# Projections in quarters at even distances, checks moved to the last groups, and a shorter lead-in, in a fused graph attention and graph convolution kernel

## Chip, core and metric

The kernel runs on one core of one Trainium2 chip. Its time is the device time of one execution in microseconds (us), given as a median of several runs. The core has five engines: PE (matrix multiplication), DVE (vector), ACT (activation functions), POOL (general purpose) and SP, which here issues DMA transfers. DVE and ACT read what PE leaves in PSUM; POOL does not.

## What is computed

Layer 0 is an attention over a graph of N = 2708 nodes with D = 128 features, with 128 "slices" of 8 components each; then come a residual, a layer norm and a two-step graph convolution. Only the attention matters here:

```python
q = (x @ Wq.T).reshape(d, n, h)      # d = 128 slices, n = 2708, h = 8
k = (x @ Wk.T).reshape(d, n, h)
v = (x @ Wv.T).reshape(d, n, h)
a = jnp.einsum('dnh,dmh->dnm', q, k) * scale
a = a + spatial_encoding + edge_encoding      # both are adj
a = jax.nn.softmax(a, axis=2)
out = jnp.einsum('dnm,dmh->dnh', a, v)
```

The reshape mixes tokens and slices. 128 tokens of x (a chunk) give 128 x 128 rows of q, k and v, in the order in which the slices use them; four slices need 4 x 2708 = 10832 rows. So the first chunk of tokens (16384 rows) holds all that the first four slices need, the second is first needed by the next four, and so on.

## The kernel before, in words

**Groups and steps.** Four slices are a group (`GB`), and there are 32 groups. A group goes through six blocks of 452 queries, and a block through 9 steps of a plan, so a group has 54 steps and the kernel 1728. A step has two to four **pieces** and one **two-exponential chunk**. A piece is two 128 x 452 tiles of transposed scores: PE multiplies (`score`, L415, into the PSUM tile `s`, two buffers), DVE adds the adjacency (`add_near`, L422, into a part of `e`, five buffers), and after the last piece ACT takes exp(2 x) of all of them in one instruction (L518). For the chunk named in `TWO_EXP`, three of the four tiles go another way: PE leaves scores in the PSUM tile `p`, ACT takes the exponential (L515, into `w`), and POOL multiplies by a ready exp(2 adj) (L516, `w<-w,ecol`). PE then multiplies `e` and `w` by the values (`add_up`, L432 to L440), and DVE copies a finished block out (`hand_on`, L446).

**exp(2 adj).** In group 0 ACT computes it, one 128 x 452 tile a step (`first_exp`, L397), and SP stores it to DRAM (`near_exp`); later groups load it (`ecol`). `look_at_near` (L404) takes, on DVE, the minimum of each of the 54 tiles in groups 0 to 3 and the maximum in groups 4 to 7. At the end, both decide with other checks whether a slower, safer attention has to be run.

**Projections.** Those of the first two token chunks (`FIRST = 2`) run before all else, K, Q and V in turn. The other 20 chunks are cut into halves of 512 columns, 120 in all, placed "amid" the steps: every sixth step in group 0, and before steps 2, 10, 18 and 26 of each later group. A half is one matmul call (two matmuls in the trace, L343) into an `s` buffer, an eviction on DVE (L345), for K and Q a cast and a subtraction on POOL (L356, L357) and two stores by SP (L352), for V one store (L347). These jobs stand in a list; one is taken at the second piece of each step. The last job of a half loads the weights of the next (L335, tile `wc`, one buffer).

**Other loads.** SP issues all DMAs, in program order: adjacency tiles eight loads ahead (`load_adj`), queries of the next block, and over the 54 steps of a group the keys and values of the next group (`load_keys`, 16 DMAs into 8 partitions each, at even steps to 30; `load_values`). POOL reorders the keys at odd steps from 33 to 49 (`order_keys`, L262) and spreads the values at steps 50 to 53.

**Order.** The order of the work on PE is not by hand: `interleave` is a planner that keeps a rough clock of PE, ACT, DVE and POOL from constants (the cost of a score, a product, a projection) and yields pieces, products and projections. The engines then run in that order and wait on semaphores.

The functions that the diff touches, with line numbers:

Of the kernel before, what the change touches and what calls it, by code (L numbers as in the profile page):

```python
# [18 lines left out]
P = 128  # L19
H = 8  # L20
# [19 lines left out]
def interleave(plan, blocks, short, amid=(), bufs=4, patience=0.1):  # L40
# [10 lines left out]
    PROJECT, TAKE, SPLIT = 0.95, 0.7, 1.25  # L51
# [91 lines left out]
def graph_attention_gcn(ctx: ExitStack, tc: tile.TileContext, x, xT, adj, adjT, adjP, adjS,  # L143
# [45 lines left out]
    with ExitStack() as s:  # L189
# [58 lines left out]
        def load_keys(g, h):  # L248


            if h == 0:
                groups[g] = kpool.tile([P, NU, P], F32R, tag="k", name="k"), k_short[g % 2], vals[g % 2], v_short[g % 2]
                raw_keys[g] = raw.tile([P, N], F32R, tag="k_raw", name="k_raw")
            nc.sync.dma_start(raw_keys[g][ds(H * h, H), :].bitcast(F32),
                              ks[ds(H * (h % 4 // 2), H), ds((GB * g + h // 4) * N, N)])
# [26 lines left out]
        def load_q(g, b):  # L282
            n0, nw = QBS[b]
            q = queries[g, b] = qpool.tile([P, QB], F32R, tag="q", name="q")
            for j in range(GB):
                for i in range(2):
                    nc.sync.dma_start(q[ds(32 * j + 2 * H * i, 2 * H), :nw].bitcast(F32),
                                      qs[:, ds((GB * g + j) * N + n0, nw)])
# [31 lines left out]
        assert GB * N <= FIRST * P * P  # L320
        halves = [(c, i, h) for c in range(FIRST, NM) for i in range(3) for h in range(2)]
# [6 lines left out]
        def load_half(n):  # L328
            c, i, h = halves[n]
# [4 lines left out]
            given[c, i, h] = proj.tile([P, NB], F32, tag="wc", name="wc")  # L334
            nc.sync.dma_start(given[c, i, h], projections[i][0][:, ts(h, NB)])  # L335

        def project(n):

            c, i, h = halves[n]
# [3 lines left out]
            nc.tensor.matmul(pp[:mi, 0, :], given[c][:, :mi], given.pop((c, i, h)), start=True, stop=True)  # L343
            a = proj.tile([P, NB], F32, tag="pa", name="pa")[:mi]
            nc.vector.tensor_scalar_mul(a, pp[:mi, 0], half_scale if i == 1 else 1.0)  # L345
            if i == 2:
                return [lambda: nc.sync.dma_start(dst.rearrange("(i g) e -> i (g e)", g=P)[ds(i0, mi), ts(h, NB)], a)]  # L347
            o = proj.tile([P, 2, NB], F32R, tag="pr", name="pr")[:mi]

            def store():  # L350
                for l in range(2):
                    nc.sync.dma_start(dst.rearrange("r (i g) -> i r g", g=P)[ds(i0, mi), ds(H * l + 4 * h, 4)],  # L352
                                      o[:, l].bitcast(F32).rearrange("p (e g) -> p e g", g=P))


            return [lambda: nc.gpsimd.tensor_copy(o[:, 0], a),  # L356
                    lambda: nc.gpsimd.tensor_sub(o[:, 1], a, o[:, 0].bitcast(F32)), store]  # L357
# [6 lines left out]
        for n in range(ahead):  # L364
            load_adj(n)
        load_half(0)
        for i, (_, dst) in enumerate(projections):
            for c in range(FIRST):
                pp = ps.tile([P, 2, NB], F32, tag="s", name="s")
                for h in range(2):  # L370
                    nc.tensor.matmul(pp[:, h, :], first_x[:, ts(c, P)], first_w[:, ts(2 * i + h, NB)], start=True, stop=True)
                o = flat(epool.tile([P, 8, QB], F32, tag="e", name="e"))[:, : 4 * NB].rearrange("p (l f) -> p l f", l=2)
                if i == 2:
                    nc.scalar.copy(o[:, 0], flat(pp))
                    nc.sync.dma_start(dst.rearrange("(i g) e -> i (g e)", g=P)[ts(c, P)], o[:, 0])
                else:
                    f = half_scale if i == 1 else 1.0
                    nc.scalar.mul(o[:, 0].bitcast(F32R), flat(pp), f)
                    nc.vector.scalar_tensor_tensor(o[:, 1].bitcast(F32R), flat(pp), f, o[:, 0], ALU.mult, ALU.subtract)
                    nc.sync.dma_start(dst.rearrange("r (i g) -> i r g", g=P)[ts(c, P)],  # L380
                                      o.rearrange("p l (e g) -> p (l e) g", g=P))
            if i == 1:
                for h in range(16):
                    load_keys(0, h)
                load_q(0, 0)
        for j in range(GB):
            load_values(0, j)
        for h in range(9):
# [4 lines left out]
        def first_exp(b, m):  # L393
# [3 lines left out]
            nc.scalar.activation(t[:, :nw], adj_cols[0, b, -1 - m][:, :nw], AF.Exp, scale=2.0)  # L397
# [3 lines left out]
        def look_at_near(g, b, m):  # L401
            x = TWO_EXP.index(m)
            if g < 8 and g % 4 == x % 4:
                nc.vector.tensor_reduce(ends[:, g // 4, ds(b * len(TWO_EXP) + x, 1)], exp_cols[g, b, m][:, : QBS[b][1]],  # L404
                                        AX.X, (ALU.min, ALU.max)[g // 4])
# [45 lines left out]

        amid = list(range(2, 54, 6)) + [54 * g + t for g in range(1, NG) for t in (2, 10, 18, 26)]
        amid = amid[: len(halves)]
        for g in range(1, NG):
            c = (min(NG, g + 2) * GB * N - 1) // (P * P)
            assert c < FIRST or amid[halves.index((c, 2, 1))] + 8 < 54 * g
        jobs = []
        loaded = ahead
        for what, n, c, beside in interleave(plan, len(steps) // len(plan), NU, amid, bufs=5):
            if what == "amid":  # L460
                at = amid.index(n)
                jobs += project(at)
                if at + 1 < len(halves):
                    jobs.append(lambda n=at + 1: load_half(n))
# [369 lines left out]
```

## Time and profile before

| | |
|---|---|
| median of 3 runs | 6900.82 us (6892.52 to 6908.93) |
| profiled execution, its own time | 6904.39 us |
| its span in the profile | 6902.6 us |
| lead-in, to the first POOL product | 50 us |
| attention, 32 groups | to 6561 us |
| layer norm and convolution | the last 341 us |
| busy, share of the span | PE 96%, ACT 94%, DVE 89%, POOL 83% |
| ACT busy by group | 200.2 us of 200.2 in group 29; 226.8 of 238.8 in group 0 |
| checks L404 | 108 x 0.615 us (median) on DVE, from 50.7 to 1715.3 us |
| first exponentials L397 | 54 x 0.577 us (median) on ACT, in group 0 |
| evictions of halves L345 | 120, 0.691 us each at 128 rows |

Times are from one profiled execution. A row of the profile names a line of the code, its engine, and output and input by the program's names; "idle before" and the name after an arrow are the wait just ahead of an instruction and what ended it. PE's busy time is modelled and should not be read as a share of its peak. A group is told by POOL's products: every 54th starts one.

### The profile page before, as it was taken

To read this page: it belongs to the slowest core of one execution; us is meant where nothing else is said; L and a number is where in the kernel's file an instruction comes from. 1 tells how busy PE (TensorE), PEld (TensorE's weight loads), DVE (VectorE), ACT (ScalarE), POOL (GpSimd) and SP (SyncE) were. 2 spreads that over 40 slices of the span, in tenths; PEclk is the share of its full clock that TensorE was granted. 3 is DMA by queue.
4 is the path that set the end of the run, shared out by engine and by line. 5 is a ranking of instruction groups with operands and counts; after the bars stand their busy time and mean duration, and the time that the engine had idled before them with its cause. 6 is when DMAs were issued, how large, how long until landed. Compare 5 with 4: busy or idle time off the path is not lost.

```text
span 6902.6 us, 137500 instructions
## 1 busy us (share of the span) xinstructions
PE 6641.2 (96%) x50426; PEld 1983.7 (29%) x50426; DVE 6112.2 (89%) x6307; ACT 6501.8 (94%) x3605; POOL 5761.7 (83%) x2546
## 2 busy tenths in 40 slices
PE   7999999999999999999999999999999999999979
PEld 2222222222222222222222222222222222222254
DVE  6899999999999999999999999999999999999941
ACT  7999999999999999999999999999999999999910
POOL 5888888888888989888898988889898888888800
PEclk8999999999999999999999999999999999999999
DMA  8888887878888888888878788877888887777667
GB/s 266 269 246 243 249 239 234 246 241 242 249 245 243 243 246 245 253 246 247 241 242 249 245 251 248 248 240 243 244 244 255 247 240 232 231 235 239 199 203 232
DMA packets 1143258, 1674.16 MB, mean 243 GB/s; under 512 B 148922, under 2 KB 1090366, under 8 KB 1138478
## 3 DMA queue, kind: packets, MB, share of 16 engines
q1 hardware_dynamic: 1142574, 1665.29, 79.7%
q8 instruction: 399, 6.54, 0.4%
q14 instruction: 285, 2.33, 0.1%
HBM read 1582.90 MB, written 81.80 MB: 241 GB/s over the span
## 4 chain that ended last, share of the span: by engine, by line
PE 54%; DMA 13%; DVE 12%; POOL 8%; issue 6%; ACT 4%; SPq 3%; DVEq 0%; POOLq 0%; ACTq 0%
PE acc L440 27%; PE s L415 18%; DVE e L422 11%; POOL w L516 7%; DMA col<-in_adjP 4%; PE acc L661 3%; ACT w L515 2%; DMA k_raw<-ks 2%; PE p L415 2%; ACT e L518 2%; PE acc L437 2%; DMA two<-in_adjP 2%; DMA ecol<-ne 1%; PE s L343 1%; DMA q<-qs 1%
## 5 line engine op out<-in xcount | busy, mean ns | idle before, releaser
L516 POOL TENSOR_TENSOR w<-w,ecol 128x1356 f32<-128x1356 f32 (+1 forms) x1728 | 5347.4, 3102 | 755.0 <-ACT w L515 622.6
L422 DVE TENSOR_TENSOR e<-s,col 128x904 f32<-128x904 f32 (+1 forms) x4608 | 4831.3, 1092 | 339.9 <-PE s L415 196.8
L518 ACT ACTIVATE e<-e 128x2712 f32<-128x2712 f32 (+5 forms) x1728 | 4747.6, 2747 | 17.4 <-DVE e L422 14.8
L440 PE MATMUL acc<-e,vals 128*9 128x452 f32 x20352 | 3553.2, 545 | 0.1
L415 PE MATMUL s<-q,k 32*128 32x452 f32 x10944 | 2501.3, 462 | 183.4 <-DVE e L422 117.7
L515 ACT ACTIVATE w<-p 128x1356 f32<-128x1356 f32 (+1 forms) x1728 | 2439.2, 1412 | 47.1 <-PE p L415 28.5
L415 PEld LDWEIGHTS s<-q,k 32*128 32x128 f32 x10944 | 1016.7, 182 | 3370.6 <-DVE e L422 2979.4
L440 PE MATMUL acc<-w,vals 128*9 128x452 f32 x10368 | 1622.6, 545 | 0.0
L415 PE MATMUL p<-q,k 32*128 32x452 f32 (+1 forms) x5184 | 1400.5, 446 | 18.7 <-ACT w L515 18.4
L422 DVE TENSOR_TENSOR e<-s,two 128x904 f32<-128x904 f32 (+1 forms) x960 | 1049.1, 1093 | 119.9 <-PE s L415 61.1
L440 PEld LDWEIGHTS acc<-e,vals 128*9 128x9 f32 x20352 | 452.0, 89 | 807.7 <-issue 805.8
L415 PEld LDWEIGHTS p<-q,k 32*128 32x128 f32 x5184 | 575.5, 182 | 63.9 <-ACT w L515 53.6
L440 PEld LDWEIGHTS acc<-w,vals 128*9 128x9 f32 x10368 | 200.9, 88 | 193.2 <-issue 177.5
L262 POOL CAST k<-k_raw 128x336 fp32r<-128x336 f32 x251 | 222.3, 886 | 37.6 <-DMA q<-qs 37.6
L432 PE MATMUL acc<-e,v_short 128*128 128x452 f32 (+1 forms) x384 | 197.1, 595 | 0.0
L437 PE MATMUL acc<-e,v_first 128*32 128x452 f32 (+1 forms) x1536 | 185.9, 556 | 2.5
L343 PE MATMUL s<-wc,xc 128*128 128x512 f32 (+1 forms) x240 | 136.3, 650 | 6.4 <-DMA wc<-in_WvT 3.4
L345 DVE TENSOR_SCALAR pa<-s 128x512 f32<-128x512 f32 (+1 forms) x120 | 82.9, 691 | 48.6 <-PE s L343 46.2
L446 DVE COPY o<-acc 128x452 f32<-128x452 f32 x192 | 118.9, 619 | 6.4 <-PE acc L440 6.4
L661 PE MATMUL acc<-col,xw 128*128 128x512 f32 (+2 forms) x264 | 105.5, 549 | 0.0
L555 ACT ACTIVATE sd<-mv,eps 128x1 f32<-128x1 f32 (+1 forms) x22 | 6.0, 294 | 104.5 <-DVE mv L549 104.4
L661 PE MATMUL acc<-col,hw 128*128 128x512 f32 (+2 forms) x264 | 104.1, 545 | 0.0
(84 smaller groups left out, 1069.0 us busy)
## 6 DMA issues: line engine op xcount, KB each, us to landing
col<-in_adjP SPq DMA_DIRECT2D x1965, 226.0 KB
two<-in_adjP SPq DMA_DIRECT2D x1440, 226.0 KB
ecol<-ne SPq DMA_DIRECT2D x1395, 226.0 KB
col<-in_adjP SPq DMA_DIRECT2D x393, 224.0 KB
two<-in_adjP SPq DMA_DIRECT2D x288, 224.0 KB
ecol<-ne SPq DMA_DIRECT2D x279, 224.0 KB
col<-in_adjT SPq DMA_DIRECT2D x210, 256.0 KB
k_raw<-ks SPq DMA_DIRECT2D x512, 84.6 KB
```

The source lines that it names most:

```text
L262: copy(k[:, :, ts(i, n)], t[:, ts(i, n * NU)].rearrange("p (q c) -> p c q", c=NU))
L343: nc.tensor.matmul(pp[:mi, 0, :], given[c][:, :mi], given.pop((c, i, h)), start=True, stop=True)
L415: nc.tensor.matmul(to[:, :nw], k[r, m, :], q[r], start=True, stop=True)
L422: nc.vector.tensor_add(e[:, ds(at, 2), :nw], st[:, :, :nw], a)
L432: nc.tensor.matmul(a[:, :nw], vz, e[:, t, :nw], start=False, stop=False)
L437: nc.tensor.matmul(a[ds(32 * j, 32), :nw], v_first[g % 2][:, ds(32 * j, 32)], e[:, t, :nw], start=True, stop=False)
L440: nc.tensor.matmul(a[ds(32 * j, VW), :nw], v[:, m, ds(VW * j, VW)], e[:, t, :nw], start=False, stop=(m == last_chunk))
L446: nc.vector.tensor_copy(o[:, :nw], acc.pop((g, b))[:, :nw])
L515: nc.scalar.activation(w[:, :, :nw], sp[:, :, :nw], AF.Exp, scale=2.0)
L516: nc.gpsimd.tensor_mul(w[:, :, :nw], w[:, :, :nw], exp_cols[g, b, two][:, :nw].unsqueeze(1).to_broadcast([P, 3, nw]))
L518: nc.scalar.activation(e[:, :at, :nw], e[:, :at, :nw], AF.Exp, scale=2.0)
L661: nc.tensor.matmul(acc[:, :nw], src[:mw, m, :], t[:mw, :nw], start=(m == 0), stop=(last is None and m == NM - 1))
```

## The change

1. **Quarters.** Halves become quarters of 256 columns, 240 of them, each put at step 2 + 32 n // 5 for n = 0 to 239, so every 6.4 steps to step 1531 (in group 28). Cast and subtraction of a quarter become one job; the load of the next stays the last job. The planner's constants for a projection are changed.
2. **Checks.** The minimum of exp(2 adj) is taken in the last three groups, 18 tiles in each. In place of the maximum, `first_exp` has ACT give the sum of each row with the exponential (`accum_out`).
3. **Lead-in.** Only chunk 0 is projected ahead of the first loads of keys and queries. Half of these loads are issued on ACT's queue. The projections of chunk 1 come after the loads of values. Of the eight adjacency loads ahead, two go out before the projections and six after V of chunk 0 is stored.

The diff, cut to its core:

```diff
-    PROJECT, TAKE, SPLIT = 0.95, 0.7, 1.25
+    PROJECT, TAKE, SPLIT = 0.5, 0.36, 1.0
...
-        def load_keys(g, h):
+        def load_keys(g, h, queue=nc.sync):
...
-            nc.sync.dma_start(raw_keys[g][ds(H * h, H), :].bitcast(F32),
+            queue.dma_start(raw_keys[g][ds(H * h, H), :].bitcast(F32),
...
-        assert GB * N <= FIRST * P * P
-        halves = [(c, i, h) for c in range(FIRST, NM) for i in range(3) for h in range(2)]
+        assert GB * N <= P * P
+        quarters = [(c, i, h) for c in range(FIRST, NM) for i in range(3) for h in range(4)]
+        QW = 2 * P
...
-            nc.tensor.matmul(pp[:mi, 0, :], given[c][:, :mi], given.pop((c, i, h)), start=True, stop=True)
-            a = proj.tile([P, NB], F32, tag="pa", name="pa")[:mi]
-            nc.vector.tensor_scalar_mul(a, pp[:mi, 0], half_scale if i == 1 else 1.0)
+            nc.tensor.matmul(pp[:mi, 0, :QW], given[c][:, :mi], given.pop((c, i, h)), start=True, stop=True)
+            a = proj.tile([P, QW], F32, tag="pa", name="pa")[:mi]
+            nc.vector.tensor_scalar_mul(a, pp[:mi, 0, :QW], half_scale if i == 1 else 1.0)
+
+            def load():
+                if n + 1 < len(quarters):
+                    load_quarter(n + 1)
+
             if i == 2:
-                return [lambda: nc.sync.dma_start(dst.rearrange("(i g) e -> i (g e)", g=P)[ds(i0, mi), ts(h, NB)], a)]
-            o = proj.tile([P, 2, NB], F32R, tag="pr", name="pr")[:mi]
+                to = dst.rearrange("(i g) e -> i (g e)", g=P)[ds(i0, mi), ts(h, QW)]
+                return [lambda: nc.sync.dma_start(to, a), load]
+            o = proj.tile([P, 2, QW], F32R, tag="pr", name="pr")[:mi]
+
+            def split():
+
+                nc.gpsimd.tensor_copy(o[:, 0], a)
+                nc.gpsimd.tensor_sub(o[:, 1], a, o[:, 0].bitcast(F32))
...
-            return [lambda: nc.gpsimd.tensor_copy(o[:, 0], a),
-                    lambda: nc.gpsimd.tensor_sub(o[:, 1], a, o[:, 0].bitcast(F32)), store]
+            return [split, store, load]
...
-        for n in range(ahead):
+        for n in range(2):
             load_adj(n)
-        load_half(0)
-        for i, (_, dst) in enumerate(projections):
-            for c in range(FIRST):
...
-            if i == 1:
-                for h in range(16):
-                    load_keys(0, h)
-                load_q(0, 0)
+
+        def project_all(c, i):
...
+        for i in range(2):
+            project_all(0, i)()
+        store_v = project_all(0, 2)
+        for h in range(16):
+            load_keys(0, h, nc.scalar if h % 2 else nc.sync)
+        load_q(0, 0, (nc.sync, nc.scalar))
+        store_v()
+        for n in range(2, ahead):
+            load_adj(n)
         for j in range(GB):
             load_values(0, j)
+        for i in range(3):
+            project_all(1, i)()
+        load_quarter(0)
         for h in range(9):
             order_keys(0, h, (nc.gpsimd.tensor_copy, nc.vector.tensor_copy, nc.scalar.copy)[h % 3])
...
-            nc.scalar.activation(t[:, :nw], adj_cols[0, b, -1 - m][:, :nw], AF.Exp, scale=2.0)
+            x = b * len(TWO_EXP) + TWO_EXP.index(m)
+            nc.scalar.activation(t[:, :nw], adj_cols[0, b, -1 - m][:, :nw], AF.Exp, scale=2.0,
+                                 accum_out=ends[:, 1, x : x + 1])
...
             x = TWO_EXP.index(m)
-            if g < 8 and g % 4 == x % 4:
-                nc.vector.tensor_reduce(ends[:, g // 4, ds(b * len(TWO_EXP) + x, 1)], exp_cols[g, b, m][:, : QBS[b][1]],
-                                        AX.X, (ALU.min, ALU.max)[g // 4])
+            if x % 3 == g - NG + 3:
+                nc.vector.tensor_reduce(ends[:, 0, ds(b * len(TWO_EXP) + x, 1)], exp_cols[g, b, m][:, : QBS[b][1]],
+                                        AX.X, ALU.min)
...
-        amid = list(range(2, 54, 6)) + [54 * g + t for g in range(1, NG) for t in (2, 10, 18, 26)]
-        amid = amid[: len(halves)]
+        amid = [2 + 32 * n // 5 for n in range(len(quarters))]
```

`project_all(c, i)` does for one chunk and one of K, Q and V what the two loops did: two matmuls, ACT's eviction, DVE's remainder for K and Q; it returns the store, so that it can be issued later.

## Prediction

> **What bounds the kernel now.** I first read the page's busy shares: PE 96%, ACT 94%, DVE 89%, POOL 83%; four candidates. PE's ends are modelled, and the page's chain gives PE 54%, which can't separate engines that feed each other. So I cut the attention into its 32 groups, at the starts of every 54th POOL product (L516), and asked for the busy time of each engine in such stretches: group 0, group 1, group 4, two groups in which only projections are added (8 and 24), and group 29, which has neither projections nor checks.
>
> ```profile
> core 0: us, PE busy (x) PEld busy (x) DVE busy (x) ACT busy (x) POOL busy (x), PEclk, DMA share, GB/s
> 50.30:289.10 238.80, 213.23 (x1510) 58.90 (x1512) 199.10 (x208) 226.82 (x162) 188.27 (x89) 0.95 0.90 276
> 289.10:492.30 203.20, 198.68 (x1550) 56.38 (x1542) 192.55 (x197) 201.32 (x109) 179.30 (x79) 1.00 0.84 255
> ...
> 904.80:1111.00 206.20, 196.78 (x1541) 55.27 (x1537) 194.18 (x202) 202.62 (x109) 179.28 (x79) 1.00 0.80 240
> ...
> 1723.90:1925.80 201.90, 197.69 (x1546) 55.98 (x1538) 186.28 (x185) 200.55 (x109) 180.75 (x81) 1.00 0.81 245
> 4952.70:5154.60 201.90, 197.87 (x1542) 56.64 (x1538) 186.06 (x184) 200.60 (x109) 180.92 (x81) 1.00 0.84 247
> ...
> 5961.40:6161.60 200.20, 193.41 (x1534) 57.43 (x1530) 182.43 (x180) 200.20 (x109) 175.71 (x75) 1.00 0.77 234
> ```
>
> The first number is the span. In group 29 ACT is busy 200.20 of 200.20 us: **ACT's exponentials are the floor**, 200.2 us a group. Groups 8 and 24 (four halves of a projection each) take 201.9: 1.6 us over the floor, so a half costs about 0.38 us of ACT's time, though ACT does nothing for it. Groups 1 to 7 also hold the checks (L404) and take 203.2, 208.0, 204.5, 206.2, 202.9, 205.5 and 204.5 us, 1434.8 in sum, where seven at 201.8 would be 1412.6. In group 0 ACT also does the 54 exponentials of L397.
>
> How a half reaches ACT is in the timeline of PE, then of DVE and ACT, in group 25:
>
> ```profile
> 5216.06 1.13 PE L343 MATMUL s<-wc,xc 128*128 128x512 f32 x2
> 5217.11 0.47 PE L415 MATMUL s<-q,k 32*128 32x452 f32 x2
> ...
> 5217.22 0.69 DVE L345 TENSOR_SCALAR pa<-s 128x512 f32<-128x512 f32 x1 [0.48 <-PE s L343]
> ...
> 5222.46 3.22 ACT L518 ACTIVATE e<-e 128x3616 f32<-128x3616 f32 x1 [0.80 <-DVE e L422]
> ```
>
> A half holds PE for 1.05 us (5216.06 to 5217.11); DVE idles 0.48, then evicts for 0.69 (0.61 to the next start). That is 1.09 us of DVE's lead, and 4 us later ACT has idled 0.80. Elsewhere a half costs ACT nothing: the lead decides.
>
> The start, in the stretches and in the DMA queue's timeline:
>
> ```profile
> 21.00:27.00 6.00, 0.00 (x0) 0.00 (x0) 0.00 (x0) 0.79 (x1) 0.00 (x0) 0.83 1.02 289
> 27.00:35.00 8.00, 0.00 (x0) 0.00 (x0) 0.00 (x0) 0.00 (x0) 0.00 (x0) 0.50 0.50 88
> 35.00:43.00 8.00, 0.00 (x0) 0.00 (x0) 0.64 (x2) 0.67 (x1) 0.61 (x1) 0.50 0.46 82
> ...
> 20.97 13.79 SPq L254 DMA_DIRECT2D k_raw<-ks  x16
> 35.45 7.07 SPq L287 DMA_DIRECT2D q<-qs  x8
> 42.33 1.68 ACT L262 CAST k<-k_raw 128x336 fp32r<-128x336 f32 x2 [20.55 <-DMA q<-qs]
> ```
>
> Until 27 the DMA engines are full (289 GB/s), with stores of chunk 1 too; then half of them are busy with 8-partition key loads, and ACT waits 20.55 us.
>
> **What the Trainium skill says.** "ScalarE: Activation LUTs", section "What ACT_TABLE_LOAD costs", prices an ACTIVATE with immediates at 186 ns + 0.833 ns an element, overlapping by about 93 ns back to back. For 1356 elements that is 1.32 us; the ACT timeline has 1.30. For L397's 452 it is 0.56; the trace's median is 0.577. No page that I found prices ACT's accumulator output. "DMA: Bandwidth & Descriptors", section "Issuing engines are not separate DMA queues", says that a second issuing engine saves only issue time. The half-full DMA engines above, with SP issuing on, fit that.
>
> **The change, part by part.** A minus is a gain.
>
> **Checks.** 108 reduces of 0.615 us go. In groups 1 to 7 they were what put these groups above group 8: 1434.8 - 1412.6 = **-22**. In group 0 ACT covers them: nothing. 54 minimum reduces come to groups 29 to 31, 18 each: 11.1 us of DVE a group. DVE idles there for 200.2 - 182.4 = 17.8 us, but in the fullest group (1) it still idled 203.2 - 192.6 = 10.6, so 7.2 us are free: 11.1 - 7.2 = 3.9 us over. Group 4 (18 reduces and four halves, 6.0 over the floor, 1.6 of it for the halves) says 4.4 at most; group 1 (12 reduces, 3.0 - 1.6 = 1.4) scaled by 18/12 says 2.1. I take 3.3 a group: **+10** (6 to 13).
>
> **accum_out on L397.** The trace has no such form on ACT. Below: 0, if the sum rides along. Above: a second short instruction with its 186 ns and the lost overlap, about 0.28. A gain is excluded, since the same elements pass. I take 0.15: 54 x 0.15 = **+8** (0 to 15), all on ACT's path in group 0.
>
> **The start.** K, Q and V of chunk 0 remain ahead of the loads; chunk 1 (stores of 1.0, 1.0 and 0.5 MB) goes behind them. The key loads no longer stand behind chunk 1's 2 MB: at 289 to 350 GB/s that is 6 to 7 us. With half of the loads on ACT's queue the two may overlap more, but they use the same engines; I credit nothing and leave up to 8 us for the range. What is moved: on SP the six later adjacency loads stand behind store_v, and chunk 1's stores (7 us of DMA) stand ahead of the first step's loads; the eight tiles loaded ahead last over two steps of 4.3 us. On ACT 12 issues, then three evictions of 1.0 us (L378, L374), and on DVE two of 1.23 (L379), stand ahead of the casts of order_keys; they fall in the 20 us in which both idle, and if that cover goes they cost up to 3. I take **-7** (0 to -15).
>
> **Late weights in group 0.** Here ACT lost 5.17 us once and 2.7 a second time; the waits of 150 to 166 us name the cause, the load of the next half:
>
> ```profile
> PE s L343 <- DMA wc<-in_WvT: 3.4, 1, 3.4
> ```
>
> Cast, subtraction, store, load took a step each and halves were 6 steps apart; now cast and subtraction share a step, so the load goes out a step (4.3 us) earlier. **-6** (0 to -8). In later groups the load came 12 to 20 us after its matmul, and 6 steps of 3.7 are 22; one step less leaves 6 to 14 us to land in, which should do.
>
> **Quarters.** 120 halves become 240 quarters, one per 6.4 steps rather than at t = 2, 10, 18 and 26 of 54. A quarter's PE time is half of 0.86 plus the 0.2 around it, 0.6 us. Its eviction is 0.69 - 256 x 1.06 ns = 0.42 (1.06 ns an element: L422's 1.094 for 904 against L404's 0.616 for 452). The next scores need about 0.7 us from the freed buffer, so DVE loses some 0.75 a quarter, not 0.42: per group 8.4 x 0.75 = 6.3 us against 4 x 1.09 = 4.4. That still fits into the 7.2 us of room, so what counts is the stall per piece. At the phases of the 9-step pattern where halves sit, they cost ACT 0.41, 0, 0.83 and 0 us; taking 0.34 of disturbance off leaves 0.07, 0, 0.49, 0: mean 0.14. Proportional to DVE's loss it would be 0.38 x 0.75/1.09 = 0.26. I take 0.18: 240 x 0.18 = 43 us against 120 x 0.38 = 45: **-2** (from -40 at no stall to +46 at the halves' own price). POOL's split is about 1.1 us per K or Q quarter (0.61 + 1.29 per half before), and now also meets order_keys (0.89 us, t = 33 to 49); POOL idles 20 us a group, which covers it on average. The added descriptors (1 KB rows for 2 KB) are small beside 1,143,258 packets.
>
> **Sum:** -22 + 10 + 8 - 7 - 6 - 2 = -19. The profiled execution took 6904.4 us (span 6902.6), so 6885; it stands 3.6 above the median of 6900.8, so the median would be about **6882**.
>
> **Rivals.**
> - **Each quarter costs ACT what a half did** (the slower side). PE and DVE pass the scores through two buffers; any piece takes one and breaks that rhythm, whatever its width, and there are twice as many. Place: ACT's waits before L515 and L518, groups 1 to 28. Price: 240 x 0.38 = 91 instead of 43, total +29: 6930. For it: DVE's 0.75 is nearly a half's loss. Against: PE is held half as long. It decides from about 0.38 us; break-even is (45 + 17)/240 = 0.26, slower by over 0.2% above 0.32.
> - **Even spacing hides all**: 0.04 a piece, 10 us, total -52: 6849. For it: the stalls at two of four places were zero. Against: the quarters meet all nine phases.
> - **The start gains nothing and group 0's stall stays**: the loads remain bound by the half of the DMA engines, and chunk 1's stores delay the first steps instead. Total -6: 6895.
> - **DVE has no room in the last groups**: 3 x 11.1 = 33 instead of 10, total +4: 6905.
>
> **How the numbers follow.** About 0.2% (14 us) is what a measurement of this kernel can tell from no change. Forecast 0.46, quarters at the old price 0.20, all hidden 0.24, no gain at the start 0.06, no room 0.04. The forecast's own range, from 0.10 to 0.26 us a quarter, is 6863 to 6901; 0.30 of it lies beyond -14. Faster: 0.30 + 0.24 + 0.02 (no gain at the start) = 0.56; same: 0.16 + 0.04 + 0.04 + 0.01 = 0.25; slower: 0.19, all from the first rival. The range runs from 6844 to 6927, which takes in the hidden case, most of the costly one and the unknown price of the accumulator.
>
> **What would show it.** Groups 1 to 7 at the length of group 8. Groups 29 to 31 at 203 to 204 us, DVE busy 193. Group 0 with 54 more ACT records or L397 longer than 0.577. First cast near 35 us instead of 42.3. No 5 us gap of ACT in group 0. Groups 8 to 27 between 201.2 and 202.3: if they stand near 203.3, the first rival holds and the sum is wrong by its largest term; at 200.5, the second.

## The result, and the profile after

| | before | after |
|---|---|---|
| median of ten runs each, us | 6900.81 (6892.52 to 6908.93) | 6884.83 (6876.89 to 6889.57) |
| ratio of times, 95% interval | | 0.9976 (0.9966 to 0.9986) |
| profiled execution, us | 6904.39 | 6884.26 |
| its span, us | 6902.6 | 6882.5 |

The kernel became 16 us faster by the medians, 20.1 by the two profiled executions. The forecast was 6882 and 6885. The first question is whether the 20 us lie where the sum put them, so the attention is cut again at every 54th POOL product. The first number of each row below is the stretch, the second its length; then busy time of PE, PE's weight loads, DVE, ACT and POOL, the clock, the DMA share and GB/s. The rows are group 0, groups 1, 4, 8 and 24, then the last three (29, 30, 31). Line numbers are those of each kernel: in the changed one a score is L438, the addition of the adjacency L445, the product with the values L463, ACT's exponentials L534 (`w`) and L537 (`e`), the first exp(2 adj) L418, a quarter's matmul L344 and eviction L346, a reduce L427 and a block's copy L469.

```profile
core 0: us, PE busy (x) PEld busy (x) DVE busy (x) ACT busy (x) POOL busy (x), PEclk, DMA share, GB/s
45.60:284.60 239.00, 211.17 (x1518) 60.62 (x1516) 190.80 (x190) 230.25 (x215) 184.57 (x91) 0.95 0.90 275
...
284.60:486.20 201.60, 198.13 (x1562) 57.20 (x1554) 186.62 (x189) 200.83 (x109) 180.91 (x85) 1.00 0.82 252
888.60:1091.00 202.40, 199.16 (x1560) 56.93 (x1556) 187.23 (x190) 201.04 (x109) 182.92 (x89) 1.00 0.79 244
1696.20:1897.10 200.90, 198.01 (x1550) 56.76 (x1546) 186.48 (x189) 200.49 (x109) 179.77 (x83) 1.00 0.82 248
4926.50:5127.50 201.00, 198.09 (x1550) 56.77 (x1546) 186.59 (x189) 200.58 (x109) 182.99 (x89) 1.00 0.80 247
5933.40:6133.50 200.10, 192.63 (x1526) 55.90 (x1528) 191.01 (x197) 200.10 (x109) 175.62 (x75) 1.00 0.78 234
6133.50:6334.40 200.90, 192.18 (x1534) 54.24 (x1530) 191.36 (x199) 200.90 (x109) 175.61 (x75) 1.00 0.76 232
6334.40:6541.20 206.80, 194.44 (x1545) 53.33 (x1541) 187.49 (x194) 200.73 (x107) 167.03 (x54) 0.98 0.61 195
```

Groups 1 and 4 now look like 8 and 24. In groups 29 and 30 ACT is busy all the time although DVE has 18 reduces more; group 31 alone is clearly long. "Start" is from here on the first POOL product plus the length of group 0, that is, the time at which group 1 begins. As a balance, in us:

| stretch | before | after | difference | the forecast's terms for it |
|---|---|---|---|---|
| the start: up to the first product, and group 0 | 50.1 + 238.8 | 45.5 + 239.0 | -4.4 | -7 start, -6 late weights, +8 sums |
| groups 1 to 7 | 1434.7 | 1411.5 | -23.2 | -22 checks |
| groups 8 to 27, mean | 201.81 | 201.85 | +0.9 in sum | -2 quarters, with the row below |
| group 28 | 201.3 | 200.2 | -1.1 | |
| groups 29 to 31 | 200.2, 200.2, 199.8 | 200.1, 200.9, 206.8 | +7.6 | +10 reduces |

The rows add up to -20.2. Two terms hide more than they tell: the first row is a sum of opposite parts, and the "3.3 us a group" of the forecast turned out to be one group with nearly all of it.

In group 0, ACT's timeline after the change (start, duration; in brackets the idle time before and what ended it) and then the waits from 45 to 62 us:

```profile
32.42 1.94 ACT L388 ACTIVATE e<-s 128x1024 fp32r<-128x1024 f32 x2 [18.17 <-DMA q<-qs]
38.57 1.01 ACT L385 COPY e<-s 128x1024 f32<-128x1024 f32 x1 [4.21 <-PE s L382]
39.48 1.68 ACT L262 CAST k<-k_raw 128x336 fp32r<-128x336 f32 x2
...
44.12 1.30 ACT L534 ACTIVATE w<-p 128x1356 f32<-128x1356 f32 x1 [1.50 <-PE p L438]
...
49.47 0.56 ACT L418 ACTIVATE ecol<-col 128x452 f32<-128x452 f32 x1
49.94 0.19 ACT L418 ACTIVATION_READ_ACCUMULATOR ecol<-col 128x1 f32 x1
50.03 1.28 ACT L534 ACTIVATE w<-p 128x1356 f32<-128x1356 f32 x1
...
61.45 1.30 ACT L534 ACTIVATE w<-p 128x1356 f32<-128x1356 f32 x1 [7.98 <-PE s L438]
```

```profile
PE s L344 <- DMA wc<-in_WkT: 7.5, 1, 7.5
```

The keys came early: POOL's first cast is at 34.93 us (42.4 before; 35 was forecast). But ACT stands in its own queue of DMA issues until 32.42, then has chunk 1's evictions ahead of its casts, to 39.48. POOL meanwhile stands for the values:

```profile
43.89 0.33 POOL L279 COPY vals<-v_raw 128x168 f32<-128x168 f32 x1 [5.82 <-DMA v_raw<-vs]
...
45.52 3.07 POOL L535 TENSOR_TENSOR w<-w,ecol 128x1356 f32<-128x1356 f32 x1
```

ACT's `w` is ready at 45.42 (44.12 + 1.30), and POOL goes from the values straight to the product at 45.52, so two things hold the first product to the same moment. It is only 4.5 us earlier than before. Then one gap of 7.98 us: PE waits 7.5 us for the weights of the first quarter. They are issued at 50.57, behind chunk 1's stores in SP's queue:

```profile
44.00 0.40 SPq L390 DMA_DIRECT2D ks<-e  x1
44.49 1.62 SPq L390 DMA_DIRECT2D qs<-e  x1
46.20 3.08 SPq L386 DMA_DIRECT2D vs<-e  x1
49.34 1.18 SPq L334 DMA_DIRECT2D xc<-in_xT  x1
50.57 1.24 SPq L336 DMA_DIRECT2D wc<-in_WkT  x1
```

The second row of ACT's L418 above is the price of `accum_out`: a record of its own, here 0.19 us (0.25 in the median of the 54), of which the next instruction overlaps half (it starts at 50.03, 0.09 after 49.94).

### The profile page after: what moved, and what is told of

The parts are those of the page before. It is cut to its first block, busy times and chain, and to the rows that moved or that the text cites. A ratio compares the mean times of both kernels' runs of the same rounds, so it can differ in the third digit from the quotient of the medians.

```text
span 6882.5 us, 138849 instructions
## 1 busy us (share of the span) xinstructions
PE 6655.3 (97%) x50666; PEld 2002.7 (29%) x50666; DVE 6106.7 (89%) x6373; ACT 6505.4 (95%) x3659; POOL 5789.3 (84%) x2706
## 4 chain that ended last, share of the span: by engine, by line
PE 58%; DMA 11%; DVE 11%; POOL 6%; issue 5%; ACT 5%; SPq 4%; DVEq 0%; ACTq 0%; POOLq 0%
PE acc L463 29%; PE s L438 18%; DVE e L445 10%; POOL w L535 6%; DMA col<-in_adjP 4%; PE acc L680 3%; DMA two<-in_adjP 3%; ACT e L537 3%; PE p L438 2%; PE acc L455 2%; SPq L287 2%; ACT w L534 2%; DMA ecol<-ne 2%; PE s L344 1%; PE acc L460 1%
## 5 line engine op out<-in xcount | busy, mean ns | idle before, releaser
L445 DVE TENSOR_TENSOR e<-s,col 128x904 f32<-128x904 f32 (+1 forms) x4608 | 4817.2, 1091 | 320.6 <-PE s L438 130.3
L537 ACT ACTIVATE e<-e 128x2712 f32<-128x2712 f32 (+5 forms) x1728 | 4593.8, 2658 | 9.3 <-DVE e L445 4.3
L463 PE MATMUL acc<-e,vals 128*9 128x452 f32 x20352 | 3561.9, 545 | 0.4 <-ACT e L537 0.4
L438 PE MATMUL s<-q,k 32*128 32x452 f32 x10944 | 2475.2, 462 | 120.9 <-DVE e L445 93.3
L534 ACT ACTIVATE w<-p 128x1356 f32<-128x1356 f32 (+1 forms) x1728 | 2286.0, 1323 | 33.9 <-PE p L438 20.4
L438 PEld LDWEIGHTS s<-q,k 32*128 32x128 f32 x10944 | 997.6, 182 | 3267.6 <-DVE e L445 2845.5
L463 PE MATMUL acc<-w,vals 128*9 128x452 f32 x10368 | 1622.0, 544 | 0.0
L438 PE MATMUL p<-q,k 32*128 32x452 f32 (+1 forms) x5184 | 1328.1, 444 | 21.2 <-ACT w L534 19.6
L445 DVE TENSOR_TENSOR e<-s,two 128x904 f32<-128x904 f32 (+1 forms) x960 | 1048.3, 1092 | 126.5 <-PE s L438 81.3
L463 PEld LDWEIGHTS acc<-e,vals 128*9 128x9 f32 x20352 | 441.7, 88 | 786.2 <-issue 773.7
L438 PEld LDWEIGHTS p<-q,k 32*128 32x128 f32 x5184 | 547.1, 182 | 51.0 <-ACT w L534 45.3
L463 PEld LDWEIGHTS acc<-w,vals 128*9 128x9 f32 x10368 | 207.0, 88 | 175.8 <-issue 160.3
L344 PE MATMUL s<-wc,xc 128*128 128x256 f32 (+1 forms) x480 | 166.4, 428 | 8.9 <-DMA wc<-in_WkT 7.5
L469 DVE COPY o<-acc 128x452 f32<-128x452 f32 x192 | 119.9, 624 | 40.0 <-PE acc L463 39.8
L360 POOL TENSOR_TENSOR pr<-pa,pr 128x256 fp32r<-128x256 f32 (+1 forms) x160 | 117.8, 736 | 12.8
L346 DVE TENSOR_SCALAR pa<-s 128x256 f32<-128x256 f32 (+1 forms) x240 | 100.2, 418 | 27.6 <-PE s L344 23.9
L344 PEld LDWEIGHTS s<-wc,xc 128*128 128x128 f32 (+1 forms) x480 | 70.5, 184 | 133.4 <-DVE e L445 116.4
```

Source lines behind the costliest of these rows:

```text
L344: nc.tensor.matmul(pp[:mi, 0, :QW], given[c][:, :mi], given.pop((c, i, h)), start=True, stop=True)
L438: nc.tensor.matmul(to[:, :nw], k[r, m, :], q[r], start=True, stop=True)
L445: nc.vector.tensor_add(e[:, ds(at, 2), :nw], st[:, :, :nw], a)
L463: nc.tensor.matmul(a[ds(32 * j, VW), :nw], v[:, m, ds(VW * j, VW)], e[:, t, :nw], start=False, stop=(m == last_chunk))
L534: nc.scalar.activation(w[:, :, :nw], sp[:, :, :nw], AF.Exp, scale=2.0)
L537: nc.scalar.activation(e[:, :at, :nw], e[:, :at, :nw], AF.Exp, scale=2.0)
```

## Experiments

All times are medians with the ratio to the kernel before and its 95% interval. Each ran with the kernel before beside it; 1 to 4 shared a chip, 5 to 8 another and 9 to 12 a third. Stretches come from one profiled execution of each kernel. Groups 8 to 27 take from 201.72 to 202.05 us on average in the ten kernels that leave the quarters' work on PE and DVE as it is and add nothing to these groups, which is how far apart two kernels may stand there by chance.

**1. The checks where they were.** `c_old_checks`: the quarters and the lead-in of the change stay.

```diff
-            if x % 3 == g - NG + 3:
-                nc.vector.tensor_reduce(ends[:, 0, ...], ..., ALU.min)
+            if g < 8 and g % 4 == x % 4:
+                nc.vector.tensor_reduce(ends[:, g // 4, ...], ..., (ALU.min, ALU.max)[g // 4])
...
-                                 accum_out=ends[:, 1, x : x + 1])
```

> The changed kernel with its checks put back: 108 reduces in groups 0 to 7, no sum with the exponentials. Theory (moving the checks is the main gain, and the new reduces in the last groups are nearly covered): groups 1 to 7 grow by 18 to 22 us in sum, group 0 loses about 5 us, groups 29 to 31 fall back to 200.2 each; total 8 to 16 us above the changed kernel, 0.9989 to 1.0000 of the kernel before. Rival (the gain came from the quarters' even spacing, and the checks' price in groups 1 to 7 was that of bunched halves beside them): groups 1 to 7 grow by less than 8 us and the kernel stays within 3 us of the changed one.

6908.15 us, 1.0011 (1.0004 to 1.0018): 23 above the change's median. Groups 1 to 7, the changed kernel's first, then this one's:

```profile
284.60:1696.20 1411.60, 1386.84 (x10844) 398.82 (x10836) 1306.51 (x1320) 1405.65 (x757) 1271.48 (x599) 1.00 0.81 248
```

```profile
288.69:1726.51 1437.82, 1390.84 (x10844) 394.81 (x10836) 1349.78 (x1410) 1412.04 (x757) 1271.59 (x599) 1.00 0.80 243
```

DVE has 90 instructions and 43 us more, and the stretch is 26.2 us longer. Groups 29 to 31 fall by 7.8, to 600.0. Without the move of its checks the change is slower than the kernel before: the quarters and the lead-in bring nothing together.

**2. No reduces in the last groups.** `c_no_reduces` leaves out the 54 minimum reduces.

```diff
-            if x % 3 == g - NG + 3:
-                nc.vector.tensor_reduce(ends[:, 0, ...], ..., ALU.min)
+            return
```

> The changed kernel without its 54 minimum reduces in groups 29 to 31 (the minimum is not looked at; its place holds ones). As predicted (18 reduces overflow DVE's room by 3.3 us a group): groups 29 to 31 fall by 10 us in sum. Rival (ACT stayed busy through groups 29 and 30 with the reduces, so DVE had the room; what the last group lost was the TensorE clock's dip): groups 29 and 30 stay at 200 to 201, and the total falls by 0 to 3 us.

6883.79 us, 0.9975 (0.9964 to 0.9985). Group 31 went back to

```profile
6334.90:6534.60 199.70, 193.02 (x1534) 57.34 (x1530) 182.02 (x181) 199.70 (x109) 167.33 (x57) 1.00 0.64 207
```

and groups 29 to 31 to 599.9, 7.9 less than in the changed kernel. The median shows only 1 us of it; in the profiled execution the start happened to be 5.8 longer (290.3 against 284.5), which hides it there. The reading by groups is the evidence here; the medians, with an interval 14 us wide, neither confirm it nor speak against it.

Why only group 31? Part of the answer is the clock. In the changed kernel (four stretches around 6410 us):

```profile
6403.20:6406.60 3.40, 3.30 (x37) 0.69 (x30) 3.11 (x3) 3.40 (x3) 2.21 (x2) 1.00 0.85 241
6406.60:6410.00 3.40, 2.23 (x25) 0.80 (x22) 2.94 (x4) 3.40 (x3) 3.40 (x2) 0.98 0.11 40
6410.00:6416.80 6.80, 6.80 (x33) 1.19 (x29) 4.45 (x5) 4.82 (x3) 5.36 (x2) 0.51 0.46 129
6416.80:6420.20 3.40, 3.29 (x33) 0.92 (x29) 2.81 (x3) 2.53 (x2) 1.16 (x1) 1.00 0.98 289
```

The timelines of DVE, PE and ACT around it:

```profile
6408.08 0.61 DVE L427 TENSOR_REDUCE ends<-ecol 128x1 f32<-128x452 f32 x1
...
6409.62 0.62 DVE L469 COPY o<-acc 128x452 f32<-128x452 f32 x1
```

```profile
6409.75 0.65 PE L438 MATMUL s<-q,k 32*128 32x452 f32 x2 [1.06 <-DVE e L445]
```

```profile
6417.67 1.30 ACT L534 ACTIVATE w<-p 128x1356 f32<-128x1356 f32 x1 [2.85 <-PE s L438]
```

Read in order: a reduce and a block's copy, with one addition between them, delay DVE, PE waits 1.06 us for a score buffer, and from 6406.6 to 6410 it is busy 2.23 of 3.40 us. The next 6.8 us run at half clock (0.51), scores take 0.74 us for 0.47, and ACT idles 2.85.

Where the reduce stands in the block differs between the three groups. In group 31 it comes 1.54 us ahead of the copy; in group 30 it is 4.7 us ahead (the lines below), and in group 29 the nearest one comes 2.5 us after the copy:

```profile
6202.77 0.61 DVE L427 TENSOR_REDUCE ends<-ecol 128x1 f32<-128x452 f32 x1
...
6207.48 0.62 DVE L469 COPY o<-acc 128x452 f32<-128x452 f32 x1
```

PE's waits in groups 29, 30 and 31 (in us: total, times, longest), each from its own stretch:

```profile
PE s L438 <- DVE e L445: 6.0, 15, 0.5
...
PE s L438 <- DVE e L445: 7.0, 17, 0.5
...
PE s L438 <- DVE e L445: 10.3, 17, 1.1
```

In all eleven kernels with these reduces PE waits 1.05 to 1.07 us six times in group 31, once a block and for the first time within 8 us of the group's start, and never over 0.54 in groups 29 and 30. In the three without them (before, `c_old_checks`, `c_no_reduces`) it never waits over 0.54 in group 31 either. So the place of the reduce fits what group 31 loses; no run moves it.

The Trainium skill, "TensorE: Matmul & The Clock Gate", section "What's actually happening", tells of windows of 3413 ns and of half the clock after an idle one. Here the window was two thirds full, not idle. I cut groups 31 into windows of that length in all 14 profiled kernels. In the three without the reduces no window there is busy less than 0.84 and the clock doesn't halve. In the eleven with them there are 40 windows at 0.65 to 0.69, after 19 of which the clock halves; it never halves after a fuller one there. The one kernel of these in which it didn't is `l_early_both`:

```profile
6336.28:6538.48 202.20, 190.14 (x1545) 53.08 (x1541) 187.19 (x194) 200.60 (x107) 167.25 (x54) 1.00 0.61 199
```

The others follow the time at half clock: with 3.4 us of it group 31 takes 203.8, with 6.8 us 205.2 to 205.3 (five kernels), with 10.2 us 206.5 to 206.7 (three), with 13.7 us 208.3. So the reduces alone cost 2.5 us here (202.2 against 199.7), and the clock about 1.5 us more for every 3.4 us that it is halved. Why half of the windows at 0.66 are forgiven stays open.

**3. No row sums.** `c_no_sum` leaves out the accumulator output.

```diff
-            nc.scalar.activation(..., AF.Exp, scale=2.0, accum_out=ends[:, 1, x : x + 1])
+            nc.scalar.activation(..., AF.Exp, scale=2.0)
```

> The changed kernel without the row sums of the first exponentials (their place holds ones). Predicted price 0.15 us each: 8 us less in group 0. Rival from the trace of the changed kernel (the accumulator read lasts 0.19 us but the next instruction starts 0.09 after it): 54 x 0.09 = 4.9 us less. Third: group 0 waits for something else there, 0 us.

6884.1 us, 0.9977 (0.9968 to 0.9985). From the start of an L418 to the next instruction, where that follows at once, the median is 0.47 us here and in the kernel before, and 0.56 in the changed kernel: 54 x 0.09 = 5.0 us of ACT. Yet the start is 284.9 against 284.5. In this lead-in group 0 isn't ACT's (8.75 us idle), so the time may simply be absorbed; but starts vary by several us, and one profiled execution of each can't show that none of it arrives.

**4. Halves at even distances.** `q_even_halves` has 120 halves, one per 12.8 steps, cast and subtraction in one job as in the change.

```diff
-        quarters = [... for h in range(4)]; QW = 2 * P
+        quarters = [... for h in range(2)]; QW = 4 * P
...
-        amid = [2 + 32 * n // 5 for n in range(len(quarters))]
+        amid = [2 + 64 * n // 5 for n in range(len(quarters))]
...
-    PROJECT, TAKE, SPLIT = 0.5, 0.36, 1.0
+    PROJECT, TAKE, SPLIT = 0.95, 0.7, 1.25
```

> The changed kernel with its projections in halves of 512 columns again (and the planner's constants for halves), but at even distances of 12.8 steps, 120 pieces. If a half costs ACT 0.38 us wherever it stands (width sets the price, as the forecast had it): groups 8 to 27 at about 201.8, total as the changed kernel. If what matters is the distance to the next piece and not the width (each piece costs about 0.2): groups 8 to 27 at 201.0, total about 20 us less than the changed kernel. If a wider piece at the nine phases hits worse than at the four old places: above 202, total 5 or more us more.

6894.62 us, 0.9991 (0.9983 to 0.9999). Its groups 8 to 27 take 201.95 on average, (201.95 - 200.2)/4.22 = 0.41 us a half; before it was 0.40, and a quarter costs (201.85 - 200.2)/8.44 = 0.20. So spacing brings nothing that can be seen beside the spread of 0.33 us, and the price goes with the width. The other 10 us against the change lie mostly in the start (291.6), where ACT has one gap of 10.32.

**5. The first quarter's weights early.** `l_early_weights` moves one call.

```diff
         for n in range(2):
             load_adj(n)
+        load_quarter(0)
...
             project_all(1, i)()
-        load_quarter(0)
```

> The changed kernel with the loads for the first quarter (its tokens and weights) issued with the first two adjacency loads instead of behind chunk 1's stores. If ACT's 8 us gap at the second step of group 0 comes from these weights (theory): the gap falls to about 2 us, total 6 us less than the changed kernel, about 0.9967 of the kernel before. If the gap is set by chunk 1's stores or the adjacency loads behind them: it stays at 5 us or more and the total is as the changed kernel's.

6883.97 us, 0.9977 (0.9967 to 0.9986). The gap of 7.98 is gone and nothing is won. ACT's timeline:

```profile
55.90 1.30 ACT L534 ACTIVATE w<-p 128x1356 f32<-128x1356 f32 x1 [0.62 <-PE s L438]
...
60.44 0.58 ACT L418 ACTIVATE ecol<-col 128x452 f32<-128x452 f32 x1 [0.88 <-DMA col<-in_adjP]
...
71.14 0.58 ACT L418 ACTIVATE ecol<-col 128x452 f32<-128x452 f32 x1 [2.37 <-DMA col<-in_adjP]
```

The wait for weights has become waits for adjacency tiles. The theory that the late weights are what the new lead-in costs falls: here the adjacency tiles that SP issues after chunk 1's stores are late instead.

**6. Chunk 1's arithmetic ahead of the loads, its stores behind.** `l_early_both`, on top of 5.

```diff
         store_v = project_all(0, 2)
+        stores = [project_all(1, i) for i in range(3)]
...
-        for i in range(3):
-            project_all(1, i)()
+        for store in stores:
+            store()
```

> The same with early weights, and with chunk 1 also computed (PE, ACT, DVE) before the key loads are issued; its stores stay where they were. Theory (ACT waits in its own queue for the last query load and only then evicts chunk 1, which stands ahead of its casts): the first addition comes 3 to 4 us earlier, near 38.5 us, total 9 to 10 us less than the changed kernel, 0.9962 of the kernel before. If ACT's later issue of its half of the key loads costs the same again: first addition at 41 to 42, total as with early weights alone.

6884.84 us, 0.9977 (0.9969 to 0.9985). Start 287.5. The DMA share from 50 to 100 us (next to last number) is now 0.99:

```profile
50.00:100.00 50.00, 45.03 (x265) 11.57 (x263) 34.14 (x36) 42.54 (x40) 33.14 (x15) 0.74 0.99 298
```

Moving the arithmetic brings nothing: ACT's `w` for the first step is ready at 47.5 us, but POOL, which waits for the values until 48.45, starts the first product at 50.1. What is left of the new lead-in are the place of the stores, the six later adjacency tiles and the second queue.

**7. The old lead-in under the new rest.** `l_old_lead`: both chunks first, all eight adjacency tiles and the first weights ahead, all loads on SP.

```diff
-        for n in range(2):
+        for n in range(ahead):
             load_adj(n)
+        load_quarter(0)
...
         for i in range(2):
-            project_all(0, i)()
+            for c in range(2):
+                project_all(c, i)()
...
         for h in range(16):
-            load_keys(0, h, nc.scalar if h % 2 else nc.sync)
...
+            load_keys(0, h)
+        load_q(0, 0)
+        for c in range(2):
+            project_all(c, 2)()
...
```

> The changed kernel with the lead-in of before: both chunks projected first, all loads on SP, the first weights loaded early. By the prediction's term for the start it loses 7 us; by the two traces (first product 4.5 us later, but the gap at the second step 6 us shorter) it gains 1 to 2 us and stands within 3 us of the changed kernel.

6879.96 us, 0.9972 (0.9961 to 0.9983). Group 0, then 50 to 100 us:

```profile
47.50:279.20 231.70, 211.46 (x1518) 60.69 (x1518) 191.15 (x190) 230.37 (x215) 184.49 (x91) 0.96 0.87 272
50.00:100.00 50.00, 46.51 (x318) 12.65 (x316) 40.15 (x41) 49.54 (x49) 36.93 (x17) 0.91 0.86 268
```

ACT is idle 1.3 us in all of group 0, where the changed kernel idles 8.75, and from 50 to 100 us the DMA engines have 14% left where that one has 5%. (The kernel before, with this lead-in but with halves in group 0, has 6%.) The first product is at 47.5 against 45.5: the keys do come later, but group 0 is 7.3 shorter. On one chip, this kernel's median is 4.0 us below that of 5 and 4.9 below that of 6, which both have the new lead-in; single executions overlap (6876 to 6885 here, 6879 to 6892 there).

**8. No split on POOL.** `q_no_split` leaves out the cast and the subtraction of K and Q quarters and stores the evicted tile in both places.

```diff
             def split():
-                nc.gpsimd.tensor_copy(o[:, 0], a)
-                nc.gpsimd.tensor_sub(o[:, 1], a, o[:, 0].bitcast(F32))
+                return
...
-                                      o[:, l].bitcast(F32).rearrange("p (e g) -> p e g", g=P))
+                                      a.rearrange("p (e g) -> p e g", g=P))
```

> The changed kernel without POOL's cast and subtraction for the quarters (K and Q are stored unsplit, twice, so the scores of groups beyond the first are not the reference's). Groups 8 to 27 stand 1.65 us above the floor of 200.2. If PE and DVE time of a piece sets that (theory): they stay at 201.6 to 201.9, total within 3 us of the changed kernel. If POOL's share does (the split delays POOL's products and with them PE): they fall to 200.2 to 200.8, total 30 us less.

6888.53 us, 0.9983 (0.9977 to 0.999); groups 8 to 27 take 201.98, inside the spread given above. POOL's part of a quarter costs nothing that can be seen.

**9. No matmul and no eviction.** `q_no_matmul` leaves out PE's and DVE's part of every quarter amid the steps and stores a constant tile; loads, split and stores stay.

```diff
-            nc.tensor.matmul(pp[:mi, 0, :QW], ...)
-            a = proj.tile([P, QW], F32, tag="pa", name="pa")[:mi]
-            nc.vector.tensor_scalar_mul(a, pp[:mi, 0, :QW], ...)
+            a = still[:mi]
```

> The changed kernel without the quarters' matmuls and evictions (POOL splits, and SP stores, a constant tile, so the scores of later groups are not the reference's; the loads of weights stay, and the planner still leaves room for the pieces). If PE and DVE time of a piece sets the 1.65 us by which groups 8 to 27 stand above the floor of 200.2 (theory, after leaving out POOL's split changed nothing): they fall to 200.2 to 200.6. If the loads and stores set it, or the gaps in the planner's order: they stay at 201.5 or more.

6853.9 us, 0.9927 (0.9913 to 0.994), 31 below the change. Group 24:

```profile
4905.58:5105.84 200.26, 197.85 (x1534) 57.59 (x1532) 184.45 (x181) 200.26 (x109) 182.79 (x89) 1.00 0.81 248
```

Groups 8 to 27 take 200.67: of the 1.65 us over the floor, 1.2 are PE's and DVE's. The other 0.47 may be the loads, the stores or the planner's places for quarters; no run separates these.

**10. The old lead-in with two queues.** `l_two_queues` is 7 with half of the key and query loads issued on ACT's queue.

```diff
-            load_keys(0, h)
-        load_q(0, 0)
+            load_keys(0, h, nc.scalar if h % 2 else nc.sync)
+        load_q(0, 0, (nc.sync, nc.scalar))
```

> The changed kernel with the lead-in of before (both chunks first, eight adjacency tiles first), but with half of the key and query loads on ACT's queue. Theory (the same DMA engines carry both queues, and what the new lead-in lost is that chunk 1's stores and six adjacency tiles left the time in which the DMA engines are half idle): first product plus group 0 at 278 to 281 us, as with the old lead-in on SP alone, total within 3 us of it. Rival (the second queue is what costs, as ACT stands in its own queue for the loads): first product plus group 0 at 284 or more.

6879.37 us, 0.997 (0.9958 to 0.9982). Start 279.2, as in 7: no gain and no loss, as the Trainium skill, "DMA: Bandwidth & Descriptors", section "Issuing engines are not separate DMA queues", has it for the transfer itself.

**11. The old lead-in without row sums.** `b_old_lead_no_sum` is 7 without the accumulator output.

```diff
-                                 accum_out=ends[:, 1, x : x + 1])
```

> The changed kernel with the lead-in of before and without the row sums (their place holds ones). With the new lead-in, leaving the sums out changed first product plus group 0 by nothing (284.9 for 284.6), since DMA set the pace there. If that is why: here, where ACT idles only 1.5 us in group 0, it falls by 54 x 0.09 = 4.9 us, from 279.2 to 274.3. If the accumulator read is hidden beside other work: it stays at 279.

6882.27 us, 0.9971 (0.9959 to 0.9982). Inconclusive: group 0 is 2.0 shorter than in 7, but the first product came at 54.0 instead of 47.5, because the same key loads ran slower. From 30 to 40 us, this kernel and then 7:

```profile
30.00:40.00 10.00, 0.00 (x0) 0.00 (x0) 0.00 (x0) 0.00 (x0) 0.00 (x0) 0.50 0.51 72
```

```profile
30.00:40.00 10.00, 0.00 (x0) 0.00 (x0) 0.25 (x1) 0.28 (x1) 0.23 (x1) 0.50 0.48 100
```

**12. The maximum spread out.** `b_spread_max` is 7 without row sums; DVE takes the maximum again, of 27 tiles in group 0 and of one in each of groups 1 to 27.

```diff
+            k = b * len(TWO_EXP) + x
+            if g == (1 + k // 2 if k % 2 else 0):
+                nc.vector.tensor_reduce(ends[:, 1, ds(k, 1)], ..., ALU.max)
```

> A full kernel: the change with the lead-in of before, and with the maximum of exp(2 adj) taken on DVE in place of the row sums, 27 tiles in group 0 and one in each of groups 1 to 27; the minimum stays in groups 29 to 31. If group 0 is bound by ACT and one reduce a group fits into DVE's idle time: group 0 as without the sums (5 us less than with them), groups 1 to 27 longer by 0 to 0.1 us each, total 2 to 5 us less than with the old lead-in alone, 0.9968 of the kernel before. If each reduce costs what the checks cost before (0.25 us): groups 1 to 27 7 us longer, total 2 us more.

6891.11 us, 0.9984 (0.9978 to 0.9991). It differs from 11 by these reduces (and a memset at the start of 11), ran on the same chip, and its median is 8.8 us higher. Groups 8 to 27 take 202.11, against 202.05 in 11 (and 201.80 in 7), so what one reduce costs a group doesn't stand out from the spread. In the profiled execution group 0 is 2.3 longer than in 11, and group 31, with three halvings, takes 208.3 against 203.8; the rest of the 8.8 isn't found. As a better version it fails.

The lead-in is the one part that the runs advise against. In nine profiled kernels with the new one (5 and 6 among them, which vary it) the start takes 284.5 to 291.6 (mean 287.9), in four with the old one, under the new rest, 279.2 to 283.8 (280.8). Kernels 7 and 10 stand about 5 us below the change by their medians, and their intervals overlap with its own; the changed kernel itself was not run beside them, only 5 and 6 were beside 7.

## Why the prediction was right, and where it wasn't

- **Checks, -22: right.** -23.2 in the traces, and putting them back costs 26.2. Reading what a stretch costs over a neighbour without the operation (1434.8 against seven times group 8) needed no model of the operation. Group 2 of the kernel before has 6.8 us at half clock, which is part of its 208.1; the reading doesn't hang on that, as `c_old_checks` has none and is no shorter (1437.8).
- **Reduces, +10: right in size by luck, wrong in mechanism.** +7.6, of which groups 29 and 30 take 0.6. The step "so 7.2 us are free" fails: in groups 29 and 30 DVE idles 9.1 and 9.5 us and ACT never, so the 10.6 of group 1 was no floor. (In group 30 the same 109 ACT instructions have 0.8 us more in their records than in group 29: a busy share of 1 can hide a small delay.) What the term lacked was where in a block a reduce meets the copy, and the clock. In `l_early_both`, where the clock doesn't halve, groups 29 to 31 are 3.3 us longer than without reduces, which is below the forecast's 6 to 13. The sign that was set, 203 to 204 us in each of the three groups, came in none. Rival 4 (no room, 33) is out.
- **accum_out, +8: mis-sized.** 0.09 each, not 0.15: 5.0 us of ACT. It is a short second record, as the upper bound assumed, and it overlaps like any other: the 0.19 of the row above less the 93 ns that the Trainium skill, "ScalarE: Activation LUTs", section "What ACT_TABLE_LOAD costs", gives for neighbours leaves 0.10. How much of it reaches the end is open: nothing is seen of it in the new lead-in (3), and in the old one (11) group 0 is 2.0 shorter without it, in one execution each.
- **Start, -7: wrong in sign.** Against the old lead-in it costs about 5 (284.5 against 279.2) to 7 (the means). Two steps failed. The cover "they fall in the 20 us in which both idle" was not there for ACT, which was held in its own queue of DMA issues until 32.42: POOL's cast came at 34.93, 7.4 earlier, and the first product only 4.5 earlier. That ACT's delay is the 3 us that the text named as the price is not shown, as the values held POOL to the same moment. And "chunk 1's stores (7 us of DMA) stand ahead of the first step's loads" was seen, but not priced. In the kernel before, chunk 1's K and Q stores (the second of each two below) went out ahead of the key loads:

```profile
11.52 3.29 SPq L380 DMA_DIRECT2D ks<-e  x2
16.08 4.79 SPq L380 DMA_DIRECT2D qs<-e  x2
```

  Now they go out at 44.00 and 44.49, into the time in which group 0 loads most (a DMA share of 0.95 from 50 to 100 us), and six adjacency tiles go out later too. Experiment 10 clears the second queue; the stores and the six tiles no run separates. Rival 3 had this mechanism; it only let the old stall stay, whereas a new one of 7.98 came.
- **Late weights, -6: right.** The gaps of 5.17 and 2.7 are gone, 7.9 in all. With the old lead-in the whole of it is visible: ACT's idle time in group 0 falls from 12.0 to 1.3 while its busy time rises by 3.6 (226.82 to 230.37). Group 0 has also lost its 18 checks there and has nine quarters where it had nine halves, so the earlier load's own part of this isn't separated.
- **Quarters, -2: right.** -0.3; 0.20 us a quarter against the 0.18 taken, 0.40 for an old half against 0.38, and 0.41 for an evenly placed one. Groups 8 to 27 at 201.85 lie between the signs that were set, 201.2 and 202.3, so rivals 1 (203.3) and 2 (200.5) are out. The route to 0.18 was poor. It averaged a guess by lead with a proportional one, and DVE's loss was mis-sized. Between 1724 and 5733 us, the gap ahead, the eviction and the gap behind add up to 0.37 + 0.69 + 0.25 = 1.31 us for a half and 0.07 + 0.42 + 0.70 = 1.19 for a quarter, not 0.75. PE puts products between a quarter and the next scores, as the timelines of PE and DVE show:

```profile
5151.24 0.70 PE L344 MATMUL s<-wc,xc 128*128 128x256 f32 x2
5151.87 0.55 PE L463 MATMUL acc<-e,vals 128*9 128x452 f32 x1
...
5152.75 0.47 PE L438 MATMUL s<-q,k 32*128 32x452 f32 x2
```

```profile
5152.08 0.41 DVE L346 TENSOR_SCALAR pa<-s 128x256 f32<-128x256 f32 x1
5153.32 1.10 DVE L445 TENSOR_TENSOR e<-s,col 128x904 f32<-128x904 f32 x1 [0.83 <-DMA v_short<-vs]
```

  The eviction took 0.41 (0.42 was forecast) and PE was held 0.63 (0.6). DVE's gap of 0.83 isn't `v_short`'s: the scores started at 5152.75. Rival 1's premise, that DVE loses nearly as much by a quarter as by a half, is thus true, and its conclusion false: ACT pays by width all the same. DVE's gaps here are not ACT's; I have no run that shows why.
- **The sum.** -19 forecast, -20.1 measured in the profiled executions. The largest term and the quarters carry it; the rest is luck. The start was forecast too good by 12 to 14 us, and the other terms of the first row (+2 in sum) too bad by nearly as much: with the old lead-in kept they come to 279.2 - 288.9 = -9.7.

## What to carry to other kernels

Price an operation by the stretch that has it against a neighbour that doesn't; that held twice here to within a few us, while estimates from idle time failed. Before a transfer is moved out of a lead-in, look at how full the DMA engines are where it goes, and at which engine must issue it: an idle engine that stands in its own DMA queue is no cover. When the same work costs nothing in one stretch and something in the next, compare where in the block it falls and whom it meets there, and look at the clock.

## What the hardware showed that I had not expected

- Half the TensorE clock for 3.4 or 6.8 us in mid-kernel, after windows of 3.4 us in which PE was two thirds busy. The kernel before has it once too, at 571 us, after a window busy 0.66. It isn't tied to the reduces: `l_early_weights` has it at 4814 us after a window at 0.51, and `q_no_matmul` at 342 and 4062 us after windows at 0.50 and 0.76 by the trace. So neither the 0.69 of group 31 nor any other share is shown as a limit.
- From 30 to 40 us, in the time of the 16 key loads with 8 partitions each, the DMA engines moved 72 to 100 GB/s in different kernels with the same old lead-in on SP's queue alone. The first product varies from 44.1 to 50.1 us under the new lead-in and from 44.3 to 54.0 under the old one, as much as the change of lead-in was to bring.
- ACT stayed busy 200.10 of 200.10 us in a group in which DVE, which feeds it, was busy 191.01.
